# The first block of an attention and feed-forward kernel: masks in the score banks, tokens over two queues, one normalisation on GpSimd, the last casts split

## The chip, the cores and the metric

The kernel runs on one core of one Trainium2 chip. The metric is the device time of one execution in microseconds; the time of a kernel is the median of several executions. The profile is one further execution, taken by the hardware profiler. The engines are TensorE (PE, with its weight loads as PEld), VectorE (DVE), ScalarE (ACT), GpSimd (POOL) and SyncE (SP, which issues transfers). A q behind an engine's name (SPq, ACTq, POOLq) is its sequencer: a transfer that it issues, or a wait.

## The reference

Eight sequences of 256 tokens with 256 features go through one cross-attention and one feed-forward network, each on a layer-normalised input and each with a residual. Scores are causal, and padded keys are masked:

```python
x = x + attn(_layernorm(x), ctx_1024, ctx_1024, mask)   # softmax(q k / 16 + masks) v
h = silu(lin(y, w1) * s1) * (lin(y, w2) * s2)           # y = _layernorm(x); 256 -> 1024
h = gelu(lin(h, h1) * hs1)                              # 1024 -> 1024
h = gelu(lin(h, h2) * hs2)                              # 1024 -> 1024
x = x + lin(h, w3) * s3                                 # 1024 -> 256
```

The weights are -1, 0 or 1 in float32; a key is masked where the integer mask is 0. Masked scores are minus infinity.

## The kernel before

The 2048 tokens are cut into four blocks `t` of 512 tokens (two sequences, four tiles of 128 tokens). Blocks 0 and 1 go through the feed-forward network as a pair, then blocks 2 and 3. The order of the instructions is written out by hand: there is no scheduler, each engine runs its list in order, and the attention of the later blocks is laid as small steps between the matmuls of the network (`stages_at`). Only the first block's attention stands alone, ahead of all matmuls of the network; its two sequences `js` = (0,) and (1,) are two generators that advance in turn, a step each. What follows tells its steps in order.

`load_block` (L106) issues the loads on SP: four token tiles `xs`, the first half of the keys `kt`, the mask `mi` as 128 equal rows of 512 integers, the second half of `kt`, and the values `vs`. Meanwhile `keep_warm` (L147) runs 11 matmuls on zeros, and GpSimd makes the identity `ident` and the causal mask `causal`.

`queries_turned` (L348): `sums` (L233) takes mean and variance of each token tile on VectorE, `normed` (L240) makes `ya` = (x - mean) / std there after ScalarE's square root. TensorE turns `ya` into a bank `pqt`, and ScalarE copies both halves of it, scaled by 1/16, to `qt`. `table` (L300) loads ScalarE's function tables ahead of their use. `mask_bias` (L309) makes `bias` for the three 128-key pieces of a sequence: the first 128 queries see one piece, the other 128 see two, and two of the three pieces get the causal mask added on GpSimd.

`stages` (L390): the scores of a sequence go into one bank `ps` of 384 columns; VectorE adds `bias` into `s` (L408) and takes two maxima `nmax` (L420); ScalarE makes exponentials and their sums (L428); TensorE turns them into `pp` (L441); VectorE copies that to `prt`; TensorE multiplies with `vs` into `pv` (L459), and VectorE divides and adds to `xs` (L467). `sums` and `normed` come again for `yf`. TensorE turns `xs` into `pxt`, runs eight more matmuls on zeros for the second sequence, and turns `yf` into `pyt`. `casts` (L483) rounds `pyt` to `hyt` on ScalarE (L488), and `rest` (L276) leaves the rounding's remainder in `lyt` on VectorE. Layer 1 (`layer`, L549, from `gated`) multiplies its weights with `hyt` and then with `lyt`.

Two pools of PSUM banks matter: `ps_at`, two banks, holds `pqt`, `ps`, `pp`, `pv` and `pxt` in turn; `ps_mm`, two banks, the zeros' products and `pyt`. GpSimd issues the weights' loads (L139) behind the last `bias`, then four one-column memsets that release the next block's loads on SP, then the loads of `h1t` and `h2t` (L637, L645).

The first steps are started like this (L980 and on):

```python
first = attention(0, ready[0])
next(first)
next(first)
next(first)
w1 = load_weight(g.w1t, "w1_")
w2 = load_weight(g.w2t, "w2_")
loaded[1] = load_block(1, nc.gpsimd)
```

Of the kernel before, what the change touches and what calls it, by code (L numbers as in the profile page):

```python
# [43 lines left out]
P = 128  # L44
# [30 lines left out]
def _network(ctx, tc, g, exact, flag):  # L75
# [27 lines left out]
    def tiles(js):  # L103
        return slice(2 * js[0], 2 * js[-1] + 2)

    def load_block(t, behind=None):  # L106
# [15 lines left out]
        for n, js in enumerate(groups(t)):  # L122
# [116 lines left out]

    def normed(src, js, mv, y, name):  # L240
        own = tiles(js)
        std = new(work, [P, NT], "std", f"sd{name}", bufs=2)
        nc.scalar.activation(std[:, own], mv[:, 1, own], AF.Sqrt, bias=eps)
        rstd = new(work, [P, NT], "rstd", f"rs{name}", bufs=2)
        nc.vector.reciprocal(rstd[:, own], std[:, own])
        for i in range(NT)[own]:
            nc.vector.tensor_scalar(
                y[:, i, :],
                src[:, i, :],
                mv[:, 0, i : i + 1],  # L250
                rstd[:, i : i + 1],
                ALU.subtract,
                ALU.mult,
            )
# [23 lines left out]

    SPANS = ((0, P), (P, 3 * P))
    SW = 3 * P

    def attention(t, result):
# [24 lines left out]
    def mask_bias(t, js, once, mi):  # L309
        bias = once("bias", "bias", [P, NB, SW])  # L310
        if t:
            nc.vector.tensor_scalar(
                bias[:, :, P:], mi.rearrange("p (j k) -> p j k", j=NB), 0.0, NEG, ALU.is_equal, ALU.mult
            )
            parts = bias.rearrange("p j (k n) -> p j k n", k=3)
            nc.vector.tensor_tensor(
                parts[:, :, 0:3:2, :],
                parts[:, :, 1:3, :],
                causal.rearrange("p (j k n) -> p j k n", j=1, k=1).to_broadcast([P, NB, 2, P]),
                ALU.add,  # L320
            )
            return bias
        for j in js:
            k0, k1 = (mi[:, j * S + k * P : j * S + (k + 1) * P] for k in range(2))
            parts = [bias[:, j, k * P : (k + 1) * P] for k in range(3)]
            nc.vector.tensor_scalar(parts[1], k0, 0.0, NEG, ALU.is_equal, ALU.mult)
            nc.gpsimd.tensor_tensor(parts[0], parts[1], causal, ALU.add)
            nc.vector.tensor_scalar(parts[2], k1, 0.0, NEG, ALU.is_equal, ALU.mult)
            nc.gpsimd.tensor_tensor(parts[2], parts[2], causal, ALU.add)
        return bias  # L330

# [15 lines left out]

    def queries_turned(t, js, once, xs, mi):  # L348

        cols = tokens(js)  # L350
        mva = once("mva", "mva", [P, nc.vector.BN_AGGR_DIM, NT], bufs=2)
        sums(xs, js, mva, f"a_{t}_{js[0]}")
        yield
        y = once("y", "ya", [P, NT, D])
        normed(xs, js, mva, y, f"a_{t}_{js[0]}")
        yield
        bias = mask_bias(t, js, once, mi)
        qt = once("qt", "qt", [P, ND, TB])
        for c, pt in turned(y, js, f"pqt_{t}_{js[0]}"):

            nc.scalar.activation(qt[:, c, cols], pt, AF.Copy, scale=1.0 / 16.0)
        table(t, js, AF.Exp)
        yield
        return qt, bias, None

    def queries_loaded(t, js, once, xs, mi):

# [22 lines left out]
    def stages(t, js, once, result, xs, kt, vs, mi):  # L390
        cols = tokens(js)
        queries = queries_turned if near(t) else queries_loaded
        qt, bias, factor = yield from queries(t, js, once, xs, mi)
        s = once("y", "s", [P, NB, SW])
        nmax = once("nmax", "nmax", [P, NB, 2])
        for j in js:
            ps = ps_at.tile([P, TB], F32, tag="at", name=f"{v}ps_{t}_{j}")
            for h, (a, e) in enumerate(SPANS):
                for c in range(ND):
# [3 lines left out]
                        rhs=kt[:, c, bass.ds(j * S, e - a)],  # L403
                        start=(c == 0),
                        stop=(c == ND - 1),
                    )
            if factor is None:
                nc.vector.tensor_tensor(s[:, j, :], ps[:, :SW], bias[:, j, :], ALU.add)  # L408
            else:
# [9 lines left out]
            for h, (a, e) in enumerate(SPANS):  # L419
                nc.vector.tensor_reduce(  # L420
                    nmax[:, j, h : h + 1], s[:, j, a:e], AX.X, ALU.max, negate=True
                )
# [3 lines left out]
        for j in js:  # L426
            for h, (a, e) in enumerate(SPANS):
                nc.scalar.activation(  # L428
                    pr[:, j, a:e],
                    s[:, j, a:e],  # L430
                    AF.Exp,
# [43 lines left out]
        if t:  # L475
            yield
        mvf = once("mvf", "mvf", [P, nc.vector.BN_AGGR_DIM, NT])
        sums(xs, js, mvf, f"f_{t}_{js[0]}")
        yield
        xst = once("xst", "xst", [P, ND, TB])  # L480
        yt = []

        def casts(values):  # L483
# [3 lines left out]
            for c, value in values:  # L487
                nc.scalar.copy(yt[0][:, c, cols], value)  # L488

# [10 lines left out]
        if near(t) or t == NBLK - 1:  # L500
            y = once("y", "yf", [P, NT, D])
            normed(xs, js, mvf, y, f"f_{t}_{js[0]}")
            table(t, js, AF.Silu)
# [592 lines left out]
```

## Time and profile before

| what | us |
| --- | --- |
| median of three runs | 358.52 (357.19 to 359.10) |
| the profiled execution, in all | 357.64 |
| its span, first to last instruction | 355.8 |
| TensorE busy in the span | 340.8 (96%) |
| first product of layer 1 (`pa` with `hyt`) starts | 21.52 |
| first product of layer 1 with `lyt` starts | 22.36 |
| 256 KB of mask: issue on SP, first use on VectorE | 3.07, 8.46 |
| first weight load issued on GpSimd | 10.48 |
| last `bias` on GpSimd ends | 10.54 |

Times inside the span count from its start; the execution's own time is 1.84 us longer than the span. The table's lower half is from the timeline, which lists an instruction, or several equal ones merged, with start, length, engine, line and `out<-in`. The mean granted clock of TensorE is 0.994.

### The profile page before, as it was taken

How to read it: one execution, taken by the hardware profiler on the slowest of the kernel's cores; microseconds unless marked ns; L12 is line 12 of the kernel's file. 1: busy time of each engine (PE TensorE's matmuls, PEld its weight loads, DVE VectorE, ACT ScalarE, POOL GpSimd, SP SyncE). 2: the span in 40 equal slices, each digit the busy share in tenths (PEclk: the TensorE clock that was granted, in tenths of full speed). 3: DMA queues.
4: the chain of work that ended last, by engine and by line, in shares of the span. 5: the costliest groups of instructions: out<-in, count | busy, mean ns of one | idle time of the engine just before them, and what ended most of it. 6: DMA issues, size and time to landing. Idle time of an engine off the chain costs nothing.

```text
span 355.8 us, 4322 instructions
## 1 busy us (share of the span) xinstructions
PE 340.8 (96%) x1512; PEld 271.3 (76%) x1512; DVE 271.8 (76%) x416; ACT 218.2 (61%) x298; POOL 41.9 (12%) x73
## 2 busy tenths in 40 slices
PE   8799999999998999999999999999997999999993
PEld 3567888778877888887888878787886888888782
DVE  5868966999598947758897687589958798676771
ACT  3558733557936755757682356456995687776730
POOL 1920000320000500023000000000010000000000
PEclk9999999999999999999999999999999999999997
DMA  6799992899497944479538312950559379860032
GB/s 191 241 322 251 263 312 106 247 310 322 143 314 242 255 118 120 118 236 316 157 100 282 124 59 88 329 173 2 177 181 317 108 224 321 258 188 0 0 114 73
DMA packets 39740, 68.54 MB, mean 193 GB/s; under 512 B 2440, under 2 KB 17568, under 8 KB 39712
## 3 DMA queue, kind: packets, MB, share of 16 engines
q0 software_dynamic: 20800, 36.70, 38.9%
q1 hardware_dynamic: 18768, 31.36, 27.4%
q8 instruction: 14, 0.23, 0.3%
q14 instruction: 14, 0.11, 0.1%
q10 hardware_dynamic: 144, 0.13, 0.1%
HBM read 55.59 MB, written 8.40 MB: 180 GB/s over the span
## 4 chain that ended last, share of the span: by engine, by line
PE 79%; DVE 9%; issue 2%; ACT 1%; POOL 1%; DVEq 0%; POOLq 0%; ACTq 0%
PE px_u L696 33%; PE px_y L696 15%; PE po L962 8%; PE p L696 7%; PE pb L555 4%; PE pa L555 4%; PE ps L400 2%; PE pv L459 2%; DVE ol L277 2%; DVE T L730 2%; ACT oh L679 1%; PE pxt L265 1%; DVE hc L569 1%; DVE hd L569 1%; PE pp L441 1%
## 5 line engine op out<-in xcount | busy, mean ns | idle before, releaser
L696 PE MATMUL px_u<-ol,a 128*128 128x512 f32 x256 | 72.8, 396 | 0.9 <-DVE ol L277 0.9
L696 PE MATMUL px_u<-oh,a 128*128 128x512 f32 x256 | 73.5, 399 | 0.0
L696 PEld LDWEIGHTS px_u<-ol,a 128*128 128x128 f32 x256 | 48.1, 188 | 12.9 <-DVE ol L277 1.7
L696 PEld LDWEIGHTS px_u<-oh,a 128*128 128x128 f32 x256 | 47.8, 188 | 10.9
L696 PE MATMUL px_y<-oh,a 128*128 128x512 f32 x128 | 35.3, 398 | 3.1 <-issue 3.1
L567 ACT ACTIVATE gate<-pa,sc 128x512 f32<-128x512 f32 x32 | 21.9, 689 | 26.3 <-PE pa L555 26.1
L696 PE MATMUL px_y<-ol,a 128*128 128x512 f32 x128 | 34.9, 394 | 0.0
L637 POOL DMA_DIRECT2D a<-S x16 | 11.9, 744 | 178.9 <-PE px_u L696 55.6
L696 PEld LDWEIGHTS px_y<-oh,a 128*128 128x128 f32 x128 | 23.8, 188 | 9.4 <-issue 3.9
L696 PEld LDWEIGHTS px_y<-ol,a 128*128 128x128 f32 x128 | 24.1, 188 | 5.7
L192 ACT ACTIVATE sign<-raw 128x1024 bf16<-128x1024 f32 x16 | 16.9, 1056 | 8.1 <-DMA raw<-h1t 7.0
L555 PE MATMUL pa<-hyt,w 128*128 128x512 f32 x64 | 20.6, 403 | 0.7 <-ACT hyt L488 0.7
L555 PE MATMUL pb<-hyt,w 128*128 128x512 f32 x64 | 19.9, 391 | 0.3 <-DVE hb L569 0.3
L555 PE MATMUL pa<-lyt,w 128*128 128x512 f32 x64 | 19.9, 392 | 0.1
L555 PE MATMUL pb<-lyt,w 128*128 128x512 f32 x64 | 19.8, 390 | 0.0
L194 DVE SCALAR_TENSOR_TENSOR sign<-raw,sign 128x1024 bf16<-128x1024 f32 x16 | 19.2, 1219 | 0.2 <-ACT sign L192 0.2
L724 ACT ACTIVATE nd<-nd,sc 128x512 f32<-128x512 f32 x16 | 10.7, 716 | 13.9 <-DVE nd L727 13.9
L696 PE MATMUL p<-oh,a 128*128 128x512 f32 x64 | 17.8, 399 | 0.2 <-DVE na L727 0.2
L696 PE MATMUL p<-ol,a 128*128 128x512 f32 x64 | 17.5, 395 | 0.0
L727 DVE TENSOR_TENSOR na<-p,na 128x512 f32<-128x512 f32 x16 | 10.9, 688 | 8.5 <-PE p L696 8.5
L277 DVE TENSOR_TENSOR ol<-nT,oh 128x1024 fp32r<-128x1024 f32 x12 | 14.5, 1220 | 3.2 <-ACT oh L679 3.1
L277 DVE TENSOR_TENSOR ol<-T,oh 128x1024 fp32r<-128x1024 f32 (+1 forms) x14 | 14.6, 1069 | 2.1 <-ACT oh L679 2.0
(168 smaller groups left out, 647.2 us busy)
## 6 DMA issues: line engine op xcount, KB each, us to landing
a<-S POOLq DMA_DIRECT2D x16, 1024.0 KB, 5.5
a<-h1t POOLq DMA_DIRECT2D x6, 1024.0 KB, 8.7
a<-h2t POOLq DMA_DIRECT2D x6, 1024.0 KB, 6.7
raw<-h1t SPq DMA_DIRECT2D x8, 512.0 KB, 4.7
raw<-h2t SPq DMA_DIRECT2D x8, 512.0 KB, 4.5
vs<-ctx_n SPq DMA_DIRECT2D x4, 512.0 KB, 7.4
q<-h1t POOLq DMA_DIRECT2D x4, 512.0 KB, 21.2
q<-h2t POOLq DMA_DIRECT2D x8, 256.0 KB, 14.5
```

The source lines that it names most:

```text
L192: nc.scalar.activation(sign, raw, AF.Sign)
L194: nc.vector.scalar_tensor_tensor(sign, raw, 1.0, sign, ALU.mult, ALU.not_equal, accum_out=count[:, n : n + 1])
L277: nc.vector.tensor_tensor(lo, value, hi.bitcast(F32), ALU.subtract)
L400: nc.tensor.matmul(ps[:, a:e], lhsT=qt[:, c, bass.ts(2 * j + h, P)], rhs=kt[:, c, bass.ds(j * S, e - a)], start=(c == 0), stop=(c == ND - 1),)
L459: nc.tensor.matmul(pv[:, h, :], lhsT=prt[:, j, bass.ds(a + k * P, P)], rhs=vs[:, 2 * j + k, :], start=(k == 0), stop=(k == n - 1),)
L555: nc.tensor.matmul(pm, lhsT=wc[:, bass.ts(o, P)], rhs=x, start=(n == 0), stop=(n == len(steps) - 1),)
L567: nc.scalar.activation(gate, pa, AF.Silu, scale=sc[:, 0, o : o + 1])
L637: nc.gpsimd.dma_start(out=a, in_=src.rearrange("(k p) n -> p k n", p=P))
L696: nc.tensor.matmul(bank, lhsT=a[:, k, bass.ts(o, P)], rhs=x[k // 2][part][:, k % 2, :], start=start and (part, k) == steps[0], stop=stop a ...
L724: nc.scalar.activation(out, src, AF.Gelu, scale=sc[:, n, o : o + 1])
L727: nc.vector.tensor_tensor(out, one, other, ALU.add)
L962: nc.tensor.matmul(po, lhsT=w3[j * QK + k][:, bass.ts(o, P)], rhs=xs_[j][k // 2][part][:, k % 2, :], start=(j == 0 and (part, k) == STEPS[0]),
```

## The change

Seven things are changed, all for the first block alone (`t` = 0).

- The tokens' third and fourth tiles are loaded from ScalarE's queue; SP issues the first two.
- The mask is loaded as one row, ahead of the keys. GpSimd turns it into a row of bfloat16 `row16` (0 or -1e30 for each of 384 columns, and 128 ones behind it) and copies `ident` and `causal` to bfloat16.
- `mask_bias` makes nothing for this block. `masks_first` puts the masks into the score banks by TensorE: ones times the row, then identity times causal mask for the two causal pieces. The scores' matmuls add to that. VectorE's add goes; maxima and exponentials read the bank.
- `pqt` comes from `ps_mm`. The second sequence's `qt` is made by VectorE, and the table of Exp is loaded after the first sequence's `qt`.
- A one-column copy on GpSimd (`passed`) reads the last `ya`; the weights' loads stand behind it.
- The first sequence's `yf` is normalised by GpSimd. Its reciprocal, on VectorE, moves ahead of the second sequence's statistics (`held`).
- The second sequence's `hyt` is cast half by ScalarE, half by VectorE.

```diff
-        mi = new(io, [P, TB], "mi", f"mi_{t}", I32)
+        mi = new(io, [P if t else 1, TB], "mi", f"mi_{t}", I32)
...
-            nc.sync.dma_start(
+            (nc.sync if t or i < 2 else nc.scalar).dma_start(
...
+        mask = g.mask[:, span]
+        nc.sync.dma_start(out=mi, in_=mask.to_broadcast([P, TB]) if t else mask)
+        for js in groups(t):
...
-            if n == 0:
-                nc.sync.dma_start(out=mi, in_=g.mask[:, span].to_broadcast([P, TB]))
...
+    masks16 = new(work, [P, 2, P], "row2", "masks16", BF16)
+    nc.gpsimd.tensor_copy(masks16[:, 0, :], ident)
+    nc.gpsimd.tensor_copy(masks16[:, 1, :], causal)
+    row16 = new(work, [1, NB, SW + P], "row", "row16", BF16)
+    nc.gpsimd.memset(row16[:, 0, SW:], 1.0)
...
-        if t == 0 and js == groups(t)[-1]:
+        if t == 0 and js == groups(t)[0 if func == AF.Exp else -1]:
             nc.scalar.activation(junk, eps, func)
...
-        for j in js:
-            k0, k1 = (mi[:, j * S + k * P : j * S + (k + 1) * P] for k in range(2))
-            parts = [bias[:, j, k * P : (k + 1) * P] for k in range(3)]
-            nc.vector.tensor_scalar(parts[1], k0, 0.0, NEG, ALU.is_equal, ALU.mult)
-            nc.gpsimd.tensor_tensor(parts[0], parts[1], causal, ALU.add)
-            nc.vector.tensor_scalar(parts[2], k1, 0.0, NEG, ALU.is_equal, ALU.mult)
-            nc.gpsimd.tensor_tensor(parts[2], parts[2], causal, ALU.add)
-        return bias
+        return None
+
+    def masks_first(t, js, mi, pss):
+        if js == groups(t)[0]:
+            keys = mi.rearrange("p (j k) -> p j k", j=NB)
+            nc.gpsimd.tensor_scalar(row16[:, :, :P], keys[:, :, :P], 0.0, NEG, ALU.is_equal, ALU.mult)
+            nc.gpsimd.tensor_scalar(row16[:, :, P:SW], keys, 0.0, NEG, ALU.is_equal, ALU.mult)
+        for j in js:
+            ps = pss[j] = ps_at.tile([P, TB], F32, tag="at", name=f"{v}ps_{t}_{j}")
+            nc.tensor.matmul(
+                ps[:, :SW], lhsT=row16[:, 0, SW:], rhs=row16[:, j, :SW], start=True, stop=True
+            )
+            for _, e in SPANS:
+                nc.tensor.matmul(
+                    ps[:, e - P : e],
+                    lhsT=masks16[:, 0, :],
+                    rhs=masks16[:, 1, :],
+                    start=False,
+                    stop=True,
+                    skip_group_check=True,
+                )
+
+    held: list = []
...
+        if t == 0 and js == groups(t)[-1]:
+            passed = new(const, [P, 1], "passed", "passed")
+            nc.gpsimd.tensor_copy(passed, y[:, NT - 1, :1])
...
-        for c, pt in turned(y, js, f"pqt_{t}_{js[0]}"):
-
-            nc.scalar.activation(qt[:, c, cols], pt, AF.Copy, scale=1.0 / 16.0)
+        for c, pt in turned(y, js, f"pqt_{t}_{js[0]}", *(() if t else (ps_mm, "mm"))):
+
+            if t or js[0] == 0:
+                nc.scalar.activation(qt[:, c, cols], pt, AF.Copy, scale=1.0 / 16.0)
+            else:
+                nc.vector.tensor_scalar(qt[:, c, cols], pt, 1.0 / 16.0, None, ALU.mult)
...
-                        start=(c == 0),
+                        start=(c == 0 and t > 0),
...
+            masked = s[:, j, :] if t else ps
+            if t and factor is None:
+                nc.vector.tensor_tensor(masked, ps[:, :SW], bias[:, j, :], ALU.add)
...
-                    nmax[:, j, h : h + 1], s[:, j, a:e], AX.X, ALU.max, negate=True
+                    nmax[:, j, h : h + 1], masked[:, a:e], AX.X, ALU.max, negate=True
...
-                    s[:, j, a:e],
+                    s[:, j, a:e] if t else pss[j][:, a:e],
                     AF.Exp,
...
+        while held:
+            held.pop()()
         sums(xs, js, mvf, f"f_{t}_{js[0]}")
+        two = len(groups(t)) > 1 and js == groups(t)[0]
+        if two:
+            y = once("y", "yf", [P, NT, D])
+            held.append(lambda: normed(xs, js, mvf, y, f"f_{t}_{js[0]}", nc.gpsimd))
...
-                nc.scalar.copy(yt[0][:, c, cols], value)
+                if t or js[0] == 0:
+                    nc.scalar.copy(yt[0][:, c, cols], value)
+                    continue
+                nc.scalar.copy(yt[0][:, 0, cols], value[:, 0, :])
+                nc.vector.tensor_copy(yt[0][:, 1, cols], value[:, 1, :])
```

In the changed kernel as built, the first sequence's exponentials wait for both of its maxima, and VectorE's half of the split cast waits for ScalarE's half. Everything behind the first block keeps its order on every engine.

More of the change, by code (lines that the diff above doesn't have):

```diff
@@ L104, in tiles @@
         return slice(2 * js[0], 2 * js[-1] + 2)
+    SPANS = ((0, P), (P, 3 * P))
+    SW = 3 * P
     def load_block(t, behind=None):
@@ L118, in load_block @@
             own = bass.ds(t * TB + i * P, step * P)
-            nc.sync.dma_start(
+            (nc.sync if t or i < 2 else nc.scalar).dma_start(
                 out=xs[:, i : i + step, :], in_=g.x[own, :].rearrange("(i p) d -> p i d", p=P)
             )
-        for n, js in enumerate(groups(t)):
+        mask = g.mask[:, span]
+        nc.sync.dma_start(out=mi, in_=mask.to_broadcast([P, TB]) if t else mask)
+        for js in groups(t):
             own = bass.ds(t * TB + js[0] * S, len(js) * S)
@@ L238, in sums, with normed @@
             nc.vector.bn_aggr(out=mv[:, :, i], in_=stats[:, i, :])
-    def normed(src, js, mv, y, name):
+    def normed(src, js, mv, y, name, engine=nc.vector):
         own = tiles(js)
@@ L246, in normed @@
         for i in range(NT)[own]:
-            nc.vector.tensor_scalar(
+            engine.tensor_scalar(
                 y[:, i, :],
@@ L277, in rest @@
         nc.vector.tensor_tensor(lo, value, hi.bitcast(F32), ALU.subtract)
-    SPANS = ((0, P), (P, 3 * P))
-    SW = 3 * P
     def attention(t, result):
@@ L309, in mask_bias @@
     def mask_bias(t, js, once, mi):
-        bias = once("bias", "bias", [P, NB, SW])
         if t:
+            bias = once("bias", "bias", [P, NB, SW])
             nc.vector.tensor_scalar(
@@ L346, in on_all, with queries_turned @@
         return got
-    def queries_turned(t, js, once, xs, mi):
+    def queries_turned(t, js, once, xs, mi, pss):
         cols = tokens(js)
@@ L352, in queries_turned @@
         sums(xs, js, mva, f"a_{t}_{js[0]}")
+        if not t:
+            masks_first(t, js, mi, pss)
         yield
@@ L364, in queries_turned, with queries_loaded @@
         return qt, bias, None
-    def queries_loaded(t, js, once, xs, mi):
+    def queries_loaded(t, js, once, xs, mi, pss):
         mva = once("mva", "mva", [P, nc.vector.BN_AGGR_DIM, NT], bufs=2)
@@ L392, in stages @@
         queries = queries_turned if near(t) else queries_loaded
-        qt, bias, factor = yield from queries(t, js, once, xs, mi)
+        pss: dict = {}
+        qt, bias, factor = yield from queries(t, js, once, xs, mi, pss)
         s = once("y", "s", [P, NB, SW])
@@ L396, in stages @@
         for j in js:
-            ps = ps_at.tile([P, TB], F32, tag="at", name=f"{v}ps_{t}_{j}")
+            if t:
+                pss[j] = ps_at.tile([P, TB], F32, tag="at", name=f"{v}ps_{t}_{j}")
+            ps = pss[j]
             for h, (a, e) in enumerate(SPANS):
@@ L403, in stages @@
                         rhs=kt[:, c, bass.ds(j * S, e - a)],
-                        start=(c == 0),
+                        start=(c == 0 and t > 0),
                         stop=(c == ND - 1),
+                        skip_group_check=(t == 0),
                     )
-            if factor is None:
-                nc.vector.tensor_tensor(s[:, j, :], ps[:, :SW], bias[:, j, :], ALU.add)
-            else:
+            masked = s[:, j, :] if t else ps
+            if t and factor is None:
+                nc.vector.tensor_tensor(masked, ps[:, :SW], bias[:, j, :], ALU.add)
+            elif t:
                 for h, (a, e) in enumerate(SPANS):
                     nc.vector.scalar_tensor_tensor(
-                        s[:, j, a:e],
+                        masked[:, a:e],
                         ps[:, a:e],
@@ L429, in stages @@
                     pr[:, j, a:e],
-                    s[:, j, a:e],
+                    s[:, j, a:e] if t else pss[j][:, a:e],
                     AF.Exp,
@@ L501, in stages @@
             y = once("y", "yf", [P, NT, D])
-            normed(xs, js, mvf, y, f"f_{t}_{js[0]}")
+            if not two:
+                normed(xs, js, mvf, y, f"f_{t}_{js[0]}")
             table(t, js, AF.Silu)
```

## The prediction

> **What bounds the kernel now.** First the busy row of the page, then the waits of TensorE, then the timeline of the first 23 us.
>
> ```profile
> PE 340.8 (96%) x1512; PEld 271.3 (76%) x1512; DVE 271.8 (76%) x416; ACT 218.2 (61%) x298; POOL 41.9 (12%) x73
> ```
>
> TensorE is busy for 96% of the span. In the stretch from 22 to 100 us it works 77.4 of 78 us, and after 22 us no wait of TensorE or VectorE is for a load, but one of 1.9 us in all. So time is won or lost nearly one for one before the first hidden layer, and I follow the chain of that stretch:
>
> ```profile
> 1.19 4.87 PE L152 MATMUL warm<-zeros 128*128 128x512 bf16 x11 [1.19 <-DVE zeros L155]
> ...
> 5.17 0.43 DVE L237 BATCH_NORM_STATS2 sta<-xs 128x6 f32<-128x256 f32 x1 [0.53 <-DMA xs<-x]
> ...
> 6.46 1.62 PE L265 MATMUL pqt<-ident,ya 128*128 128x128 f32 x8 [0.40 <-DVE ya L247]
> ...
> 7.39 1.33 ACT L361 ACTIVATE qt<-pqt 128x512 f32<-128x512 f32 x2 [1.25 <-PE pqt L265]
> ...
> 8.04 2.89 PE L400 MATMUL ps<-kt,qt 128*128 128x128 f32 x16
> 8.46 0.23 DVE L326 TENSOR_SCALAR bias<-mi 128x128 f32<-128x128 int32 x1 [0.98 <-DMA mi<-mask]
> ...
> 9.74 0.56 DVE L408 TENSOR_TENSOR s<-ps,bias 128x384 f32<-128x384 f32 x1 [0.36 <-POOL bias L329]
> ...
> 11.63 0.61 DVE L420 TENSOR_REDUCE nmax<-s 128x1 f32<-128x128 f32 x2
> ...
> 11.96 0.40 ACT L428 ACTIVATE s<-s,nmax 128x128 f32<-128x128 f32 x1 [0.31 <-DVE nmax L420]
> ...
> 13.27 2.75 PE L459 MATMUL pv<-vs,prt 128*128 128x256 f32 x12
> ...
> 16.64 0.84 DVE L467 SCALAR_TENSOR_TENSOR xs<-pv,rden,xs 128x256 f32<-128x256 f32 x2
> ...
> 17.54 0.66 PE L265 MATMUL pxt<-ident,xs 128*128 128x128 f32 x4 [1.07 <-DVE xs L467]
> ...
> 18.03 1.89 PE L152 MATMUL warm<-zeros 128*128 128x512 bf16 x8
> ...
> 19.51 0.74 DVE L247 TENSOR_SCALAR yf<-xs,mvf,rsf 128x256 f32<-128x256 f32 x2
> 19.76 1.09 PE L265 MATMUL pyt<-ident,yf 128*128 128x128 f32 x8
> ...
> 20.39 1.08 ACT L488 CAST hyt<-pyt 128x512 fp32r<-128x512 f32 x2
> 21.01 1.29 DVE L277 TENSOR_TENSOR lyt<-pyt,hyt 128x512 fp32r<-128x512 f32 x2 [0.77 <-ACT hyt L488]
> ...
> 21.52 0.74 PE L555 MATMUL pa<-hyt,w 128*128 128x512 f32 x2 [0.68 <-ACT hyt L488]
> ...
> 22.36 0.73 PE L555 MATMUL pa<-lyt,w 128*128 128x512 f32 x2
> ```
>
> The columns are start, length, engine, line, operation; the bracket is idle time and what ended it. Read downwards: the fourth token tile comes 0.53 late; the queries are turned as `ya` comes; the scores wait for `qt`; VectorE then adds the mask (0.36 late, for GpSimd's `bias`), and the second sequence's exponential starts at 11.96. Behind `pv` VectorE is the chain up to `xs` of the second sequence (17.48). Then TensorE turns it, does eight warming matmuls, and only then `pyt` (19.76, with no idle time before it). The casts follow, and the last piece is `lyt`, ending at 22.30: layer 1 has run its two `hyt` products and stands until 22.36.
>
> **The change, part by part.**
>
> *Tokens over two queues.* SP issues the four loads in 1.81 us, 0.45 each; two of them go to ScalarE's queue, ahead of its table load. There an issue takes 0.38 (the last output's row), 0.8 for two, against the 1.9 us that ScalarE idles from 2.2 to 4.14: nothing. At most the 0.53 us of idle goes; `ya` then ends near 6.95 instead of 7.48.
>
> *Mask as one row.* It takes 256 KB out of the loads (0.9 us at the 290 GB/s of that stretch). It now stands before `kt` on SP, and costs `kt`, `vs` nothing: one issue, which two moved token loads repay. It lands, I estimate, at 3.9 (issue at 1.6, plus the 2.2 us of a token tile).
>
> *Masks by TensorE.* GpSimd copies two masks and turns the row into two bfloat16 pieces, one partition of 256 and of 512 elements. Nearest rows:
>
> ```profile
> L531 POOL TENSOR_TENSOR yf<-yf,mf 128x512 f32<-128x512 f32 x2 | 2.9, 1452 | 5.5 <-DVE yf L530 5.5
> ...
> L327 POOL TENSOR_TENSOR bias<-bias,causal 128x128 f32<-128x128 f32 x2 | 0.9, 452 | 7.0 <-DVE bias L328 7.0
> ```
>
> That is 0.45 and 1.45 us for 128 and 512 elements with two inputs; one input should be cheaper (causal's select, one input, took 0.29), so 1.2 to 2.2 us: ready between 5.1 and 6.2. Six matmuls with 2 x (384+128+128) = 1280 columns then stand in front of `pqt`. Their price is the clock's. The first warming block ran 11 times 512 columns in 4.87 us (0.44 each), the second 8 in 1.89 (0.24), while PEclk shows 9 in both, so the pitch is the clock to go by. Slow, the masks cost 1.1 us, fast 0.6. Narrow windows of the trace put the step late in this execution: the transposes at 6.46 last 0.45, that at 7.81 0.27. The Trainium skill, "TensorE: Matmul & The Clock Gate" (Part 1), says that the rate rises after a busy window of about 3.4 us and that the window runs free of the kernel's start, so the step moves from run to run. By the trace alone: warming frees TensorE at 5.86, masks to 6.95, `pqt` after them, `qt` at 7.7, **0.3 late**. By the rule an early step is as likely: warming ends by 5.3, masks by 5.8, `qt` at about 6.5, **0.9 early**. I take the middle, 0.3 early, and keep both ends.
>
> *No add, maxima and exponentials from the score bank.* Before, the exponential started 1.03 us after the scores' end (10.93 to 11.96): one add, one maximum. As built it now waits for both maxima (0.61 the pair), since two engines read one bank. With 0.1 for a read from PSUM (an estimate: the 0.55 of a 384-column copy from there) and two hand-overs of 0.05, 0.8: **0.2 gained**. The transposes `pp` of the second sequence also wait for the copy of the first: in my timeline 12.8, and its last two wait for the exponential at 13.0 anyway.
>
> *Second `qt` on VectorE, exp table earlier.* VectorE takes about 0.69 (its 512-column rows) at 8.2, and the second scores begin near 9.5: hidden. The table load leaves ScalarE's chain, where it ended 0.4 before it was needed: nothing.
>
> *One normalisation by GpSimd.* Two 128x256 tiles, 0.8 each between the two rows above, 1.6 us. VectorE sheds 0.75 and the second `yf` ends earlier, but `pyt` was held by the warming matmuls, not by `yf`: no gain. It starts near 17.6 and has until 19.8, so **nothing** while a tile takes under 1.1; beyond, the excess twice. In front of it on GpSimd's queue are the weight and `h1t` loads, 6.9 us of issues (10.48 to 17.39) that now start when `ya` is done (7.1): free at about 14. The `h2t` loads behind it slip by about a microsecond; they take up to 25 us and are first needed on VectorE at 61 us or later. Weights that issue 3 us earlier meet `vs`, which is not read before 13.2. The next block's loads on SP, which wait for GpSimd's memsets behind those issues, go 3 us earlier as well; they are read at 24.8.
>
> *Last casts halved.* The rule that speaks against the change: "PSUM — Partial Sum Buffer" (section on bank collisions) says that two engines may not read one bank at once, and must be kept apart by semaphores. As built, VectorE's half waits for ScalarE's half of the same bank. By the rows of a parallel split I would write 0.54 becomes 0.4; by the rule it is 0.4 plus VectorE's 0.42 (128x384 took 0.55), and this stands on VectorE between the two `lyt`, the very instructions that end last. **0.42 lost.**
>
> *The sum.* -0.3 - 0.2 + 0.42 = -0.1; with a late clock +0.5, with an early one -0.7. Against the execution's own 357.64 that is 357.5; the median of the three runs is 358.52, 0.9 above, and a result is a median, so between 357.5 and 358.4: **358.0**. Own range 357.0 to 359.3. A change within 0.5% (1.8 us) is about what a measurement of this kernel can't tell from none.
>
> **The rivals.**
>
> *A, slower: the clock falls back before layer 1.* Place: the gap between the last warming matmul (19.76) and the first `pa` (21.52), 1.76 us with nothing but transposes. With the halved cast and a late start it grows to 2.5; if GpSimd needs 1.45 a tile (its 512 row) to 3.2. The page on the clock gate names an idle window of 3.4 us; from about there the next 3.4 us run at half rate: +1.7, on top of +0.5, and 358.52 + 2.2 = **360.7**. For it: the late step above. Against: transposes fill the gap, and 1.76 did not trip it.
>
> *B, clearly faster: the broadcast of the mask is what makes the runs differ.* Its load took 5.4 us to VectorE's use (3.07 to 8.46) where a token tile takes 2.2, and the add already waits for what follows from it. If the slowest run (359.1, 1.46 above the profiled one) is that load coming later, the change takes this away and, with an early clock, 0.7: 358.52 - 1.46 - 0.7 = **356.4**. Against: in the trace it costs only 0.36.
>
> *C: the masks come too late.* At the two-input price of 2.2 us, and a landing at 4.3, TensorE waits until 6.5 and `qt` slips 0.6 more than in the late case; +1.1 on the forecast, **359.1**, not to be told from no change.
>
> **Chances.** Forecast 0.41, A 0.22, B 0.32, C 0.05. So faster 0.32, same 0.46, slower 0.22. The range 355.9 to 360.8 takes in both at their own times; what is left out is their outer halves.
>
> **What would show it.** Right: `pqt` follows six short matmuls without idle time; exponentials start 0.8 after their scores; GpSimd's `yf` ends before the warming block; the VectorE cast stands between two `lyt`. A shows as `pa` at 0.4 us a matmul; B as `qt` before 6.8 and timed runs that lie closer together. A first `pa<-lyt` under 21.3 or over 23.5 us would make the sum wrong.

## The result, and the profile after

The changed kernel takes 361.70 us (median of six executions, 360.17 to 362.68) and the kernel before, timed beside it, 357.26 (356.69 to 359.10): a ratio of 1.0116, with a 95% interval of 1.0091 to 1.0141. It is slower by 4.4 us, and above the upper end of the forecast's range (360.8). Two single executions among the runs further down, of 687 and 1197 us, were in a slower state and are left out of every ratio and count. The profiled execution took 362.52, with a span of 360.6 and a mean clock of 0.986, against 357.64, 355.8 and 0.994 before.

The busy row of the page, after:

```profile
PE 343.8 (95%) x1517; PEld 273.9 (76%) x1518; DVE 270.4 (75%) x410; ACT 217.2 (60%) x297; POOL 46.8 (13%) x77
```

TensorE is busy for 343.8 us instead of 340.8. Of these 3.0 us the six mask matmuls that the change adds account for about 0.9 (7.60 to 8.46 below); busy time that grows by more than the work is the first sign of the clock. The timeline of the first block, after (start, length, engine, line, operation, and in the bracket the idle time before it and what ended it):

```profile
1.18 4.88 PE L158 MATMUL warm<-zeros 128*128 128x512 bf16 x11 [1.18 <-DVE zeros L161]
...
4.30 1.09 POOL L337 TENSOR_SCALAR row<-mi 1x256 bf16<-1x256 int32 x1 [1.79 <-DMA mi<-mask]
...
5.46 2.09 POOL L338 TENSOR_SCALAR row<-mi 1x512 bf16<-1x512 int32 x1
...
7.60 0.32 PE L341 MATMUL ps<-row 1*128 1x384 bf16 x1 [1.54 <-POOL row L338]
...
8.46 1.07 PE L277 MATMUL pqt<-ident,ya 128*128 128x128 f32 x8
...
9.75 4.34 PE L436 MATMUL ps<-kt,qt 128*128 128x128 f32 x16 [0.23 <-ACT qt L392]
...
14.78 0.37 ACT L466 ACTIVATE s<-ps,nmax 128x128 f32<-128x128 f32 x1 [0.41 <-DVE nmax L458]
...
16.13 2.75 PE L497 MATMUL pv<-vs,prt 128*128 128x256 f32 x12
...
20.70 2.49 POOL L259 TENSOR_SCALAR yf<-xs,mvf,rsf 128x256 f32<-128x256 f32 x2 [5.83 <-DVE rsf L257]
...
21.10 1.68 PE L158 MATMUL warm<-zeros 128*128 128x512 bf16 x7
...
23.24 0.98 PE L277 MATMUL pyt<-ident,yf 128*128 128x128 f32 x7 [0.35 <-POOL yf L259]
...
24.30 0.38 ACT L535 CAST hyt<-pyt 128x256 fp32r<-128x256 f32 x1
24.44 0.69 DVE L289 TENSOR_TENSOR lyt<-pyt,hyt 128x512 fp32r<-128x512 f32 x1 [1.50 <-ACT hyt L533]
...
25.05 0.41 DVE L536 CAST hyt<-pyt 128x256 fp32r<-128x256 f32 x1
25.50 0.69 DVE L289 TENSOR_TENSOR lyt<-pyt,hyt 128x512 fp32r<-128x512 f32 x1
...
26.24 1.09 PE L604 MATMUL pa<-lyt,w 128*128 128x512 f32 x2 [0.22 <-DVE lyt L289]
...
27.13 1.05 PE L604 MATMUL pb<-hyt,w 128*128 128x512 f32 x2
```

Read it against the rows shown of before. GpSimd needs 1.09 and 2.09 us for the two pieces of the mask row, and the row is ready at 7.55. TensorE has ended its warming at 6.06 and stands for 1.54 us. The queries are turned at 8.46 instead of 6.46. The scores take 4.34 us instead of 2.89. The second sequence's exponential starts at 14.78 instead of 11.96. At the end of the block GpSimd's `yf` takes 2.49 us for two tiles and ends at 23.19, so `pyt` waits for it. ScalarE's half of the cast ends at 24.68; VectorE's half (0.41) starts only at 25.05, as VectorE's first `lyt` ends, and the second `lyt` ends at 26.19. The first product of layer 1 with `lyt` starts at 26.24; before, it was 22.36. That start is the measure of the first block in what follows.

Even then layer 1 does not run at its old speed: `pb` takes 1.05 a pair instead of 0.62, as this line of before has it:

```profile
22.92 0.62 PE L555 MATMUL pb<-hyt,w 128*128 128x512 f32 x2
```

The time of the changed kernel, cut into stretches (start:end, length, then busy time and instructions of each engine, then PEclk, the clock that TensorE was granted):

```profile
core 0: us, PE busy (x) PEld busy (x) DVE busy (x) ACT busy (x) POOL busy (x), PEclk, DMA share, GB/s
5.94:9.35 3.41, 1.87 (x15) 1.22 (x14) 1.72 (x5) 0.39 (x2) 3.19 (x5) 1.00 0.68 208
9.35:12.76 3.41, 3.18 (x12) 2.65 (x11) 0.74 (x2) 1.83 (x3) 3.41 (x10) 0.50 1.16 336
19.59:23.00 3.41, 2.44 (x12) 1.31 (x13) 2.80 (x10) 1.77 (x3) 2.30 (x2) 1.00 1.14 312
23.00:26.41 3.41, 2.16 (x10) 1.29 (x11) 1.71 (x3) 2.15 (x6) 2.34 (x4) 1.00 1.16 253
26.41:29.83 3.42, 3.42 (x9) 2.66 (x10) 0.69 (x2) 0.69 (x1) 0.72 (x1) 0.50 1.21 245
```

Two stretches of 3.41 us run at exactly half the clock: from 9.35, which is the scores, and from 26.41, which is the start of layer 1. The two begin 17.06 us apart, five times 3.41. Ahead of each lies a stretch of the same length in which TensorE worked only 1.87 and 2.16 us; the one from 19.59, with 2.44, is followed by full rate.

The account of the profiled execution: scores start 1.71 later (8.04 to 9.75); half clock in the scores 1.45; exponentials 0.34 sooner after their scores; end of the block, from the start of `pv` to the first product with `lyt`, 10.11 instead of 9.09, 1.02 lost. That makes 3.84 of the 3.88 by which the product is late. Behind it comes 0.9 more: the second half-rate stretch costs 1.7 (an estimate: half of the 3.42 us that TensorE is busy in it), and what gives 0.8 back is not traced further. In the profiled runs below with no half-rate stretch and no long stall behind that product, the rest of the span is 332.7 to 334.0.

### The profile page after: what moved, and what is told of

Its sections match the earlier page's. It is cut to its first block, busy times and chain, and to the rows that moved or that the text cites. A ratio compares the mean times of both kernels' runs of the same rounds, so it can differ in the third digit from the quotient of the medians.

```text
span 360.6 us, 4332 instructions
## 1 busy us (share of the span) xinstructions
PE 343.8 (95%) x1517; PEld 273.9 (76%) x1518; DVE 270.4 (75%) x410; ACT 217.2 (60%) x297; POOL 46.8 (13%) x77
## 4 chain that ended last, share of the span: by engine, by line
PE 79%; DVE 11%; issue 3%; POOL 2%; ACT 2%; DMA 1%; SPq 0%; POOLq 0%; DVEq 0%; ACTq 0%
PE px_u L745 33%; PE px_y L745 15%; PE po L1011 8%; PE p L745 7%; PE pb L604 4%; PE pa L604 4%; PE ps L436 3%; PE pv L497 3%; DVE ol L289 2%; DVE T L779 2%; DVE lyt L289 1%; ACT oh L728 1%; DVE hd L618 1%; PE pp L479 1%; PE pxt L277 1%
```

## The experiments

My theory was that two causes make the loss, each with a gap in which the clock falls: the row on GpSimd, and the end of the block (GpSimd's `yf`, the split cast). Rivals: the clock has nothing to do with the gaps; the loads over two queues or the earlier weights do it. All runs are in one table; "below" counts the executions with a mean clock under 0.9935. One half-rate stretch lowers the mean by 0.0048 (half of 3.41 in 358 us). The clock also falls behind the last matmul, where it costs nothing; in before that alone makes 0.994. So an execution below has, by the ends seen here, at least one half-rate stretch in its work, while one at 0.994 or 0.995 may have one or none.

The runs were made in four sets on three chips, each with the kernel before beside it, and before itself differs: on chip 5, 27 of its 107 executions are below, on chip 6 one of 42, on chip 14 none of 11. So counts are compared only within a chip.

| run | chip | first product with `lyt`, us | profiled execution, us | ratio (95% interval) | below |
| --- | --- | --- | --- | --- | --- |
| before | 5, 6, 5, 14 | 22.36 | 357.64 | 1 | 15 of 56, 1 of 42, 12 of 51, 0 of 11 |
| changed kernel | not on record | 26.24 | 362.52 | 1.0116 (1.0091 to 1.0141) | 5 of 6 |
| row_vector | 14 | 23.54 | 361.29 | 1.0112 (1.0088 to 1.0135) | 4 of 6 |
| yf_vector | 14 | 23.72 | 358.88 | 1.0108 (1.0088 to 1.0129) | 2 of 6 |
| warm_15 | 14 | 24.68 | 359.46 | 1.0081 (1.0066 to 1.0096) | 0 of 5 |
| cast_whole | 14 | 25.91 | 362.55 | 1.0093 (1.0068 to 1.0118) | 4 of 6 |
| three_undone | 5 | 22.48 | 358.31 | 1.0033 (1.0016 to 1.0051) | 8 of 22 |
| yf_cast | 5 | 24.83 | 361.55 | 1.0088 (1.0063 to 1.0112) | 5 of 6 |
| scalar_row | 5 | 22.02 | 356.46 | 1.0029 (1.0012 to 1.0046) | 14 of 19 |
| before_no_late_warm | 5 | 22.68 | 358.11 | 1.0044 (1.0027 to 1.0060) | 19 of 22 |
| scalar_filled | 6 | 23.18 | 358.41 | 1.0023 (1.0008 to 1.0039) | 5 of 20 |
| three_filled | 6 | 22.67 | 357.72 | 1.0024 (1.0013 to 1.0035) | 2 of 18 |
| three_late | 6 | 22.40 | 357.42 | 1.0047 (1.0029 to 1.0066) | 2 of 6 |
| four_undone | 6 | 22.33 | 357.69 | 1.0028 (1.0008 to 1.0047) | 2 of 11 |
| before_yf_cast | 5 | 23.05 | 357.90 | 1.0032 (1.0016 to 1.0047) | 10 of 22 |
| four_filled | 5 | 22.53 | 357.60 | 1.0001 (0.9975 to 1.0027) | 3 of 14 |
| scalar_one_queue | 5 | 22.14 | 357.30 | 1.0011 (0.9990 to 1.0032) | 12 of 22 |

### The row on VectorE (row_vector)

```diff
-            nc.gpsimd.tensor_scalar(row16[:, :, :P], keys[:, :, :P], 0.0, NEG, ALU.is_equal, ALU.mult)
-            nc.gpsimd.tensor_scalar(row16[:, :, P:SW], keys, 0.0, NEG, ALU.is_equal, ALU.mult)
+            nc.vector.tensor_scalar(row16[:, :, :P], keys[:, :, :P], 0.0, NEG, ALU.is_equal, ALU.mult)
+            nc.vector.tensor_scalar(row16[:, :, P:SW], keys, 0.0, NEG, ALU.is_equal, ALU.mult)
```

> The changed kernel with one edit: the two instructions that make the bfloat16 mask row run on VectorE instead of GpSimd. Theory 1 (the late row and, through TensorE's idle 1.5 us, the clock cost most of the loss): the row is ready near 5 us instead of 7.55, the masks follow the warming matmuls without a wait, the scores run in about 2.9 us instead of 4.34, the first product with lyt starts near 23.3 instead of 26.2, and the time falls by about 3 us, to a ratio near 1.003 against the kernel before. Rival (the scores are slow because of the masks in their bank or of the clock's own phase): the wait of 1.5 us goes, the scores still take over 4 us, the ratio stays near 1.008. Second rival (the end of the block is what costs): under 0.7 us gained, ratio 1.010.

The timeline of this run:

```profile
4.60 0.25 DVE L337 TENSOR_SCALAR row<-mi 1x256 bf16<-1x256 int32 x1
...
4.78 0.41 DVE L338 TENSOR_SCALAR row<-mi 1x512 bf16<-1x512 int32 x1
...
5.99 0.49 PE L341 MATMUL ps<-row 1*128 1x384 bf16 x1
...
8.38 2.89 PE L436 MATMUL ps<-kt,qt 128*128 128x128 f32 x16
...
11.96 0.37 ACT L466 ACTIVATE s<-ps,nmax 128x128 f32<-128x128 f32 x1 [0.31 <-DVE nmax L458]
...
13.41 2.76 PE L497 MATMUL pv<-vs,prt 128*128 128x256 f32 x12
...
20.54 0.98 PE L277 MATMUL pyt<-ident,yf 128*128 128x128 f32 x7 [0.36 <-POOL yf L259]
...
23.54 1.20 PE L604 MATMUL pa<-lyt,w 128*128 128x512 f32 x2 [0.22 <-DVE lyt L289]
```

In the profile it is as theory 1 has it: VectorE makes the same row in 0.66 us where GpSimd took 3.18, the masks follow the warming without a wait, the scores take 2.89, and the exponential starts at 11.96, exactly as before the change. So the head of the block is even, and of the 1.18 that are left at the product 1.04 lie behind the start of `pv` (10.13 from there to the product instead of 9.09). But the timed ratio hardly moved. Of the 2.7 us gained at the product the profiled execution keeps 1.2 (361.29 against 362.52). Layer 1 runs at half clock from 23.60, as it does in the changed kernel too, and there is a new wait of TensorE, in the list of waits between 180 and 210 us (what waited, for what; us in total, times, longest):

```profile
PE pa L604 <- DVE res L629: 1.0, 1, 1.0
PE pb L604 <- DVE res L629: 0.6, 1, 0.6
```

There the residual's load came late: VectorE waited 4.8 us for it, and TensorE 1.6 us for VectorE. In all other profiled executions this load costs TensorE 0.2 us or nothing. The timed executions have no list of waits, and one of them took 361.78 us at a clock of 0.998, so that the half-rate stretches alone do not explain them. What holds them up is open. (On chip 5 the row's part shows in the timed runs: three_undone and yf_cast, below.)

### The first yf on VectorE (yf_vector), the cast whole (cast_whole)

```diff
-        two = len(groups(t)) > 1 and js == groups(t)[0]
+        two = False
```

> The changed kernel with one edit: the first sequence's yf goes back to VectorE. Theory 2 (GpSimd's 1.25 us a tile holds the last transposes by 0.4 us, and through the longer gap the clock of layer 1 falls): the transposes follow the warming matmuls, the first product with lyt starts 0.4 earlier, and layer 1 starts at full clock, 0.24 us a product: 2.0 us gained, ratio near 1.006. Without the clock's part: 0.4 gained, layer 1 still starts at 0.43 us a product, ratio 1.0105. Rival (VectorE is the chain behind the attention, and gets 0.74 us back): nothing gained or up to 0.3 lost.

```diff
-                if t or js[0] == 0:
+                if True:
                     nc.scalar.copy(yt[0][:, c, cols], value)
```

> The changed kernel with one edit: the second sequence's hyt is cast whole by ScalarE, as before the change. The forecast's term: 0.42 us gained at the first product with lyt, ratio near 1.0105. If the shorter gap also keeps the clock up for layer 1: a further 1.0 to 1.7, ratio near 1.006. Rival (the cast is hidden): no difference, 1.0116.

From the start of `pv` to the first product with `lyt` it is 10.11 in the changed kernel, 9.55 with `yf` on VectorE (14.17 to 23.72) and 9.67 with the cast whole (16.24 to 25.91): 0.56 and 0.44 gained, where 0.4 each was expected. With `yf` on VectorE `pyt` follows the warming without a wait, and in the profiled execution the scores and layer 1 run at full clock. But the ratios tell neither kernel from the changed one (the intervals overlap). One half-rate stretch more or less in an execution is larger than what was to be seen: with the cast whole four of six executions are below, and the profiled one had two, one at the scores (3.58 us) and one far behind the first block:

```profile
274.80:278.21 3.41, 1.61 (x7) 1.02 (x7) 3.41 (x4) 0.80 (x2) 0.74 (x1) 1.00 0.80 299
278.21:281.62 3.41, 3.41 (x9) 2.67 (x9) 3.14 (x4) 3.41 (x5) 0.00 (x0) 0.50 1.05 293
```

TensorE stands for 1.80 us there. The kernel before has a gap of 1.9 us at the same place (1.79 of 3.42 us busy from 273.21 on), and full rate behind it. So an edit in the first block can also change the time by where the later gaps fall in the 3.41 us pattern. For yf_vector the stretches are not all, since it took 361.85 in an execution at 0.998; this is the open point of the run above once more.

### TensorE kept busy while the row is made (warm_15)

```diff
-WARM, WARM_LATER = 11, 8
+WARM, WARM_LATER = 15, 8
```

> The changed kernel with 15 instead of 11 warming matmuls at the start, which fill TensorE's idle time before the late mask row and take nothing away of the wait for it. If the idle time is what lets the clock fall in the scores: masks still start near 7.6, but the scores take about 2.9 us instead of 4.34, and 1.4 us are gained: ratio near 1.0075. If the clock falls for another cause (the phase of the throttle, or the light work of transposes and scores): scores still over 4 us, nothing gained, or 0.3 to 0.5 lost to warming that runs past the row.

```profile
7.37 0.33 PE L341 MATMUL ps<-row 1*128 1x384 bf16 x1
...
9.52 2.89 PE L436 MATMUL ps<-kt,qt 128*128 128x128 f32 x16 [0.25 <-ACT qt L392]
...
24.68 0.73 PE L604 MATMUL pa<-lyt,w 128*128 128x512 f32 x2 [0.23 <-DVE lyt L289]
```

The masks are hardly earlier (7.37), since they still wait for GpSimd. Yet the product with `lyt` comes 1.56 sooner, for the scores run at full clock, in 2.89 us. None of the five executions is below (of the three other runs on this chip 10 of 18 are), and the five times lie within 0.7 us (359.46 to 360.12). The ratio is 1.0081 against 1.0116, near the expected 1.0075, though the two intervals overlap slightly. All but the 0.23 of the earlier masks is the clock's part.

### The gap made in the kernel before (before_no_late_warm)

```diff
-WARM, WARM_LATER = 11, 8
+WARM, WARM_LATER = 11, 0
```

> The kernel before, without the eight warming matmuls ahead of the last transposes: nothing waits for their products, so only TensorE's idle time grows. If a 3.4 us stretch with TensorE busy for under about 2.17 us is followed by one at half rate: every position of the stretches has such a one between 15 and 20 us, a half-rate stretch begins between 18 and 23 us in each execution, and 1.0 to 1.7 us are lost: ratio 1.003 to 1.005. If the clock falls only after an idle time of the whole 3.4 us, or at random: no difference, 0.999 to 1.001.

Stretches of this run, columns as above:

```profile
17.80:21.20 3.40, 2.06 (x12) 1.00 (x9) 2.80 (x10) 2.43 (x5) 1.41 (x2) 1.00 1.14 348
21.20:24.60 3.40, 2.94 (x7) 2.32 (x8) 1.05 (x2) 2.08 (x4) 0.00 (x0) 0.50 1.15 331
```

Nothing waits for the products that were taken out, and 1.6 us are lost (0.44% of 357.74). 19 of 22 executions are below, where before beside it has 15 of 56; the profiled one, at 0.994, is not counted and has the stretch shown. TensorE was busy for 2.06 of 3.40 us ahead of it. So idle time of TensorE alone, with no other work delayed, brings the loss: with warm_15 this shows the clock as a cause.

### The end of the block put into the kernel before (before_yf_cast)

The edit is the change's own for `normed`, `held` and `casts`, and nothing else.

> The kernel before with two parts of the change added alone: the first yf by GpSimd and the second hyt cast in two halves. Theory: the end of the block is late by 0.6 for GpSimd's 1.25 us a tile and by 0.4 for the second half of the cast, so that the first product with lyt starts at 23.4 instead of 22.4, whatever happens ahead of it; with the longer gap before layer 1 some executions have one more half-rate stretch: ratio 1.003 to 1.005. Rival (what the head of the block loses is all, and the end is hidden): 22.4 and ratio 1.000 to 1.001.

```profile
13.04 2.76 PE L461 MATMUL pv<-vs,prt 128*128 128x256 f32 x12
...
17.51 2.49 POOL L247 TENSOR_SCALAR yf<-xs,mvf,rsf 128x256 f32<-128x256 f32 x2 [0.30 <-issue]
...
20.05 0.98 PE L265 MATMUL pyt<-ident,yf 128*128 128x128 f32 x7 [0.26 <-POOL yf L247]
...
21.86 0.41 DVE L500 CAST hyt<-pyt 128x256 fp32r<-128x256 f32 x1
...
23.05 0.73 PE L568 MATMUL pa<-lyt,w 128*128 128x512 f32 x2 [0.23 <-DVE lyt L277]
```

From `pv` to the product it is 10.01, where the kernel before has 9.09. The product starts at 23.05 and not at the 23.4 expected, since `pv` came 0.23 sooner here. So these two parts lose 0.9 by themselves, and 1.0032 in the timed ratio. The rival, that this end is hidden, falls.

### Parts undone together (three_undone, yf_cast)

Row and `yf` on VectorE and the cast whole; and the same with the row on GpSimd.

> The changed kernel with three parts undone: the mask row is made by VectorE, the first yf by VectorE, the second hyt is cast whole by ScalarE. Theory (late row, GpSimd's yf, split cast, and the gaps in which the clock falls are the whole loss): from the run with the row on VectorE, whose first product with lyt starts at 23.5, 0.6 goes with yf and 0.4 with the cast, so that it starts at 22.5, 0.1 behind the kernel before; no 3.4 us stretch before it has TensorE busy for less than 2.17 us, no half-rate stretch follows, and the ratio is 1.000 to 1.002. Rival (there is a further loss, in the loads over two queues or in the transfers behind the block, that the three parts do not touch): the first product starts at 22.5 all the same, but the ratio stays above 1.005.

> The changed kernel with two parts undone, yf by VectorE and the cast whole; the row stays on GpSimd. Theory: the first product with lyt starts 1.0 earlier than in the changed kernel with the same clock, at about 23.5 where the scores run in 2.9 us and at 25 where they fall on a half-rate stretch (in about half of the executions); layer 1 starts at full clock. Ratio 1.004 to 1.006. Rival (the two parts matter less than the row): ratio above 1.008.

The starts came as expected, 22.48, and 24.83 where the scores fell on a half-rate stretch. The ratios are higher than I wrote, and yf_cast's is where its rival had it, over 1.008. Five of its six executions are below, and its profiled one had a second half-rate stretch at 277.73, behind 1.62 us of work. The difference of the two, 0.0055 or 2.0 us on one chip, is what GpSimd's row costs with a good end of the block, later stretches included. For three_undone something was left, 1.0033, and the next runs look for it.

### What is left: clock, weights, queues (three_filled, three_late, four_undone, four_filled)

three_filled has eight more warming matmuls in TensorE's idle times, two ahead of the first `pp`, three ahead of the second and three ahead of the second `pxt`. three_late moves the hold of the weights. four_undone also puts all token loads on SP. four_filled is that with the first five of the eight matmuls. The cut shows one piece each of the first three edits.

```diff
+            if not t:
+                keep_warm(2 + j)
             pp = ps_at.tile([P, TB], F32, tag="at", name=f"{v}pp_{t}_{j}")
...
-            nc.gpsimd.tensor_copy(passed, y[:, NT - 1, :1])
+            nc.gpsimd.tensor_copy(passed, qt[:, ND - 1, TB - 1 :])
...
-            (nc.sync if t or i < 2 else nc.scalar).dma_start(
+            nc.sync.dma_start(
```

> The kernel with three parts undone and the same eight warming matmuls. Theory (clock): the ratio falls from 1.0033 to 1.000 to 1.001, as the first product with lyt is at 22.5. Rival (a loss behind the block, which showed as about 1 us in its executions at a clock of 0.994 or more): the clock is 0.994 or more in most executions and the ratio is still 1.002 to 1.003.

> The kernel with three parts undone, with the hold of the weights' loads moved from the last ya to the second qt, so that they issue about 1.4 us later, nearer to the 10.5 us of the kernel before. Theory of the rival (earlier weight and h1t loads shift the loads behind the block and cost up to 1 us there): ratio falls from 1.0033 to about 1.001. If the loads' start has no part in it: 1.0033 as before, within 0.0015.

> The kernel with three parts undone and, fourth, all token tiles loaded on SP again. Two queues gained 0.07 us at ya in the changed kernel, so ya comes at the same time within 0.1 and the mask 0.7 later, near 4.9, still ahead of the end of warming: ratio 1.003, unchanged. Rival (the second queue lets transfers interleave, so that the first tile lands 0.6 later and the gain is lost): first statistics at 2.8 instead of 3.4, ya 0.3 earlier, ratio 1.0025 or less.

> The kernel with four parts undone, with five more warming matmuls in TensorE's idle times between the scores and the second pp. What is left of the change is then the masks by TensorE from one mask row, the exponentials from the bank, the second qt by VectorE and the earlier weights. Theory (these are worth nothing together: 0.3 gained at the exponentials, 0.3 or more lost to 1280 columns of masks ahead of pqt where TensorE still runs slowly): first product with lyt at 22.3, clock 0.994 or more in most executions, ratio 1.000 to 1.0015. Rival (masks on TensorE are a loss of 0.5 or more in most executions): ratio 1.002 or more.

```profile
5.99 0.50 PE L341 MATMUL ps<-row 1*128 1x384 bf16 x1
...
7.13 1.24 PE L277 MATMUL pqt<-ident,ya 128*128 128x128 f32 x8
...
11.15 0.59 PE L158 MATMUL warm<-zeros 128*128 128x512 bf16 x2
...
13.45 2.76 PE L499 MATMUL pv<-vs,prt 128*128 128x256 f32 x12
...
22.53 0.73 PE L606 MATMUL pa<-lyt,w 128*128 128x512 f32 x2
```

The filling does not settle what is left. Two of 18 executions of three_filled are below, but on chip 6, where before has one of 42; the 8 of 22 without filling are from chip 5. On chip 6 the runs without filling have 2 of 6 and 2 of 11. The ratio of 1.0024 is what the rival had (1.002 to 1.003 at a good clock), and its interval overlaps that of three_undone. So a loss remains though hardly any execution is below, and whether the filling gained anything is not shown. The later start of the weights gains nothing (1.0047). One queue gives the first statistics at 2.84 instead of 3.51, but VectorE then waits 0.40 for the mask and makes the row before it reads the third tile at 4.95, so that `ya` is not earlier (6.19), and the ratio stays (1.0028).

With four parts undone and the gaps filled, on chip 5 again (3 of 14 below), the ratio is 1.0001: what remains of the change is worth nothing, in an interval of 0.26% to each side. It overlaps with that of four_undone, so the five matmuls' own worth is not shown by these two. In the fence the masks start at 5.99 with TensorE still at half speed (0.50 for 384 columns, 0.33 later), and `pqt` starts at 7.13 instead of 6.46; 0.28 of that is the later `ya`, the rest the masks. The exponentials give 0.34 back. Which part holds the 0.3% of three_undone stays open.

### Towards a better version (scalar_row, scalar_filled, scalar_one_queue)

```diff
-            nc.vector.tensor_scalar(row16[:, :, :P], keys[:, :, :P], 0.0, NEG, ALU.is_equal, ALU.mult)
-            nc.vector.tensor_scalar(row16[:, :, P:SW], keys, 0.0, NEG, ALU.is_equal, ALU.mult)
+            nc.scalar.activation(row16[:, :, : 2 * P], keys, AF.Relu, bias=one, scale=-1.0)
...
-WARM, WARM_LATER = 11, 8
+WARM, WARM_LATER = 9, 8
```

> As with three parts undone, but the row is made by ScalarE, 512 elements in one instruction (one less the mask, clipped at zero; the factor -1e30 moves into the row of ones), the first 128 queries' keys are read from the same 256, and 9 warming matmuls stand at the start instead of 11. Theory: ScalarE is idle from 3.2 to 4.7, the row is ready near 5.1, VectorE gets 0.66 us back for the statistics, the masks are done near 6.2 and the scores start near 7.7 instead of 8.04 before; with the 0.3 gained at the exponentials the first product with lyt starts near 21.8, 0.5 ahead of the kernel before: ratio 0.998 to 0.999. Rival (the mask's landing, or the transposes behind the masks, hold the chain): 22.5, ratio 1.000 to 1.002.

> The kernel with the row on ScalarE, with eight more warming matmuls in TensorE's idle times of the first block: two ahead of the first pp, three ahead of the second, three ahead of the second pxt, 0.21 us each, where TensorE idles 0.43, 0.80 and 1.07. Theory (its first product with lyt comes 0.34 ahead of the kernel before, but 14 of its 19 executions have a mean clock of 0.992 or less, one half-rate stretch or more, because TensorE is busy for only 2.18 of 3.41 us between 9.2 and 14.2): with over 2.5 us busy everywhere before layer 1 most executions have 0.994 or more, the first product with lyt is not later than 22.2, and the ratio falls from 1.003 to 0.998 to 1.000. Rival (the half-rate stretches come from the gap of 1.7 us near 272, or from the chip): ratio stays near 1.003.

> The kernel with the row on ScalarE, all tiles loaded on SP, 10 warming matmuls at the start and five in TensorE's idle times between the scores and the second pp. Theory (9 were too few in some executions: in the profiled one of the filled kernel TensorE ran at 0.43 us for 512 columns until about 10 us, and the scores took 3.7 us): TensorE is at full speed before 7 us in nearly all executions, the first product with lyt starts at 21.9 to 22.2, the times lie closer together, and the ratio is 0.998 to 1.0005. Rival (the masks ahead of pqt cost what the earlier start brings): ratio 1.001 to 1.003.

The last of the three:

```profile
4.65 0.72 ACT L339 ACTIVATE row<-mi,one 1x512 bf16<-1x512 int32 x1 [2.42 <-DMA mi<-mask]
...
8.03 2.89 PE L438 MATMUL ps<-kt,qt 128*128 128x128 f32 x16
...
22.14 0.73 PE L608 MATMUL pa<-lyt,w 128*128 128x512 f32 x2
```

ScalarE makes the row in 0.72 us, and in scalar_row and here the product starts at 22.02 and 22.14, earlier than in the kernel before, though scalar_row not at the 21.8 expected. The medians do not follow, and none of the three ratios came as low as its theory had it: 14 of 19 (chip 5), 5 of 20 (chip 6) and 12 of 22 (chip 5) executions are below. The fewer ones in the middle are on the chip where before has hardly any, so they do not show that the filling works. In the profiled execution of scalar_filled TensorE did not reach full speed before about 10 us, so its scores took 3.70. No version here is shown to beat the kernel before. The five executions of scalar_row that are not below have a median of 357.13 us, the 41 such of before beside it 357.53, and all its 19 together 358.67: this points to the half-rate stretches as what takes the 0.3 us gained at the product.

## Why the prediction was wrong

**The sum.** It came to -0.1 with ends of -0.7 and +0.5; the trace has +3.88 at the first product with `lyt`, and a start over 23.5 was named as the sign that the sum is wrong. In the sum's own terms: the scores start 1.71 late where the masks were to bring them 0.3 early, the half clock in the scores (1.45) stands at nothing, and the end of the block costs 1.02 where 0.42 was written.

**Masks by TensorE** (-0.3; ends -0.9 and +0.3) is the step that failed, by its first line: GpSimd's row at 1.2 to 2.2 us because "one input should be cheaper". It took 3.18, and began at 4.30, where the landing was put at 3.9. The two rows it was priced from are additions on 128 partitions; the row here is integers compared, multiplied and turned to bfloat16 on one partition, and it costs 4.1 to 4.3 ns an element, more than the 3.5 and 2.8 of those rows. Which of these differences costs is not shown. (The end of the warming, put at 5.86, is 6.06 in the line shown, 1.19 and 4.87; that changes little.) With the row made by VectorE the term came out at the +0.3 of the late end: `qt` started at 7.72 against 7.39.

**Rival C** had this place and direction, masks too late, but a wait only until 6.5 and +1.1. TensorE waited until 7.60.

**Rival A** had the clock, at half rate for 3.4 us and a price of 1.7, and layer 1 paid just that. But it was placed only there, with gaps near 3.2 us as the condition. It also struck in the scores, after an idle time of 1.54 us, and cost 1.45 there. The second step that failed is the reading of the rule: the Trainium skill, "TensorE: Matmul & The Clock Gate" (Part 1), names an idle window of about 3.4 us, and I took it as a gap of that length. In these traces half rate followed stretches in which TensorE worked 1.87 or 2.16 of 3.41 us, with no single gap over 1.54 us in the changed kernel. Small gaps can add up, though not each such stretch is followed by half rate (last section).

**GpSimd's yf** ("nothing while a tile takes under 1.1; beyond, the excess twice"): the mechanism held, the price of a tile did not. A tile took 1.25 instead of 0.8; `pyt` waited 0.35, near twice the excess over 1.1, and yf_vector has 0.56 for the part with what follows from it.

**The split cast** (+0.42) was right in size (0.44 in cast_whole) and in place: VectorE's half stands between the two `lyt` and takes 0.41. The bank rule behind it is not shown here: ScalarE's half was done 0.37 before VectorE's began, and what VectorE was busy with was the first `lyt`.

**Exponentials** (0.2 gained) are right: 0.69 after their scores, where 0.8 was written, so 0.34 gained. The second `qt` and the earlier table cost nothing, as said, and of the earlier weights three_late shows no cost.

**Two queues** (at most 0.53): nothing. The fourth tile's wait of 0.53 went, but a tile now takes 2.8 to 3.1 us from issue to landing instead of 2.1 to 2.3, the first tile is read at 3.51 instead of 2.83, and `ya` begins at 5.83 instead of 5.90. Its second pair then takes 1.02 instead of 0.73 beside GpSimd's row, and ends later than before (7.70 against 7.48).

**Rival B**, that the broadcast makes the runs differ, falls: the changed kernel's times spread over 2.5 us as much as before, and the spread goes with the clock.

## What to carry to other kernels

Price an operation on GpSimd from a row of its own kind there, or put it on an engine for which there is one; where none is near, the upper end is the estimate. Ahead of dense matmul work, add up TensorE's busy time over every 3.4 us of the timeline: an edit that lets the sum fall below about 2.2 us can cost some 1.7 us though nothing on the chain moved, and some products on zeros in the gap are a cheap test. A step that overlaps well in one profiled execution is worth what its timed executions show, so count the low clocks in them, and compare the counts only with the kernel before on the same chip.

## What the runs showed of the hardware

- The same two instructions (1x256 and 1x512 integers to bfloat16) took 1.09 and 2.09 us on GpSimd and 0.25 and 0.41 on VectorE. ScalarE did the 1x512 form, with its own operation, in 0.72. A 128x256 float32 tile, minus mean and times a factor, took 1.25 on GpSimd and 0.37 on VectorE.
- VectorE can be slower while GpSimd works: in the changed kernel the second `ya` pair takes 1.02 beside the row on GpSimd, and 0.73 in the kernel before, beside no work there. The first pair takes 0.74 beside the same row, so what decides is open.
- Half-rate stretches last 3.41 us and lie on one grid in an execution (9.35 and 26.41 in the changed kernel). Each in the profiled executions followed a stretch with at most 2.16 of 3.41 us busy. Not each such stretch is followed by one: 1.95 us of work from 197.67 on in row_vector, 1.79 from 273.21 on in before and 2.06 from 4.16 on in before_no_late_warm were followed by full rate. What else decides is open.
- The same kernel before had 27 of 107 executions below 0.9935 on one chip and one of 42 on another. Why is open.
- One late load of the residual, at about 197 us, cost TensorE 1.6 us in one profiled execution and 0.2 or nothing in the others.
